# Two attention layers on one core: maxima and scores cut into tiles of 32 rows and 32 columns

## The chip, the cores and the metric

The kernel runs on one core of one Trainium2 chip. The metric is the device time of one execution in microseconds (us). Of the kernel before there are three timed runs: 1005.83, 1009.34 and 1009.84 us, with a median of 1009.34 us.

## The reference

A batch of 32 sequences, `x` of 256 tokens by 320 channels, goes through two cross-attention layers one after the other, each with its own context of 77 tokens by 512 channels and its own weights. Each layer has 20 heads of 16 channels. Cut to what matters:

```
q = heads(x @ Wq); k = heads(ctx @ Wk); v = heads(ctx @ Wv)      # float32
s = einsum('bhqd,bhkd->bhqk', q, k) / sqrt(16)
p = softmax(s, axis=-1)
o = merge(einsum('bhqk,bhkd->bhqd', p, v))
x = o @ Wo + bias + x
```

The reference has further branches for context tokens past the 77th. There are none, so they add nothing. Everything is float32.

## The kernel before, in words

**Units and groups.** Two sequences make a pair; 16 pairs times two layers are 32 units. The 320 channels of the two sequences of a pair are laid out as five groups of 128 rows (`NG = 5`): groups 0 to 3 hold 128 channels of one sequence each, group 4 the last 64 channels of both. A group has 256 query columns and eight heads. Its 128 rows are four quadrants of 32 rows (index `j`), and a quadrant holds two heads (index `e`), 16 rows each. 32 units of five groups make 160 calls each of `maxima`, `scores`, `products` and `divide`.

**The steps of a group.** `queries`/`queries_rest` make q with the group's rows on partitions (through `project`, line 195 with 128 rows and line 184 with 64 rows, and `project_rest`, line 213). `keys`/`keys_rest` (lines 242 and 225) make kT: twice, once for each `e`, with the other head's 16 rows multiplied by zero. Then:

- `maxima` (matmul at line 326) makes, for each quadrant `j` and each half `c` of the queries, a block of 128 queries by 154 columns (two heads by 77 keys) in bank `j` of PSUM. The queries are the stationary operand (a weight load of 32 rows by 128 columns), the keys are streamed. VectorE takes the largest value over the 77 keys (`tensor_reduce`, line 334, one for each bank).
- `turn` (once a unit, after its five maxima) transposes the maxima and writes them by small DMAs into the 16 rows of q that the masked keys leave free; `kM` is kT with -1 in one such row (`tensor_scalar_add` on GpSimd, line 257), so that the next matmul subtracts the maximum.
- `scores` (matmul at line 360) makes 77 keys by 256 queries for each quadrant `j` and head `e`: the keys are the stationary operand (32 rows by 77 columns), the queries are streamed. Quadrant `j` again writes bank `j`, head `e` the half `e` of it. ScalarE takes the exponential of each bank (line 366).
- `products` (matmul at line 380, called by `values`) multiplies by the values: 77 rows by 32 columns of weights, four column tiles beside each other; a column of ones in the values gives the sums. `divide` and `values` turn, divide and turn back (lines 392 to 414).
- `finish`/`finish_rest` (lines 195, 184, 213 again) project the result and `add` (line 421) adds bias and residual.

**Tiles of the array.** A matmul whose operands sit on 32 rows, or whose output has 32 partitions, uses only that part of TensorE's array, and matmuls on different parts can run beside each other. Before the change, `maxima` and `scores` use four row tiles (32 rows, all columns), `products`, `project_rest` and `keys_rest` four column tiles (32 columns, all rows in use), and the other matmuls the whole array, or halves of 64 rows. A float32 matmul of the code appears in the trace as two weight loads and two matmuls, so 160 x 8 calls of line 326 are 2,560 matmuls.

**The order.** The order is written out by hand: each step is put into a numbered slot (`at`), and in a slot the steps run in the order load, maxima, turn, scores, values, rest, full, last. A slot has one group's maxima (for a unit six slots ahead), one group's scores, in every other slot the values of two groups, and projections. Eight PSUM banks are handed out in turn: four to a maxima call, four to a scores call, one to each other step. TensorE takes its instructions in this order; SyncE's queue issues nearly all DMAs.

Of the kernel before, what the change touches and what calls it, by code (L numbers as in the profile page):

```python
# [52 lines left out]
B, S, C, CA, L = 32, 256, 320, 512, 77  # L53
HEADS, HD = 20, 16
P = 128
# [34 lines left out]
def xattn_kernel(ctx: ExitStack, tc: tile.TileContext, xT, cT, cP, weights, outT):  # L90
    nc = tc.nc
# [10 lines left out]
    def bank(name):  # L102
        return psum.tile([P, 512], F32, tag="bank", name=name)
# [45 lines left out]
    for i in range(2):  # L149
        m = const.tile([P, 2 * NG, 32], F32, name=f"max_{i}")  # L150
# [18 lines left out]
    def of_group(x, g):  # L169

        if g < 4:
            return x[:, (g // 2) * NT + (g % 2) * S : (g // 2) * NT + (g % 2 + 1) * S]
        return x[:, 2 * NT : NX]
# [145 lines left out]
    def maxima(u, g):  # L319
        q0, kT, mx = st[u]["q"][0], st[u]["k"], maxes[u % 2]  # L320
        q = of_group(q0, g)
        ps = [bank(f"psm_{u}_{g}_{j}") for j in range(4)]
        for c in range(S // P):
            for j in range(4):
                r = slice(32 * j, 32 * j + 32)
                nc.tensor.matmul(  # L326
                    ps[j][:, c * 2 * L : (c + 1) * 2 * L],
                    q[r, c * P : (c + 1) * P],
                    kT[r, :, g, :],
                    start=True,  # L330
                    stop=True,
                )
        for j in range(4):
            nc.vector.tensor_reduce(  # L334
                mx[:, 2 * g : 2 * g + 2, 2 * j : 2 * j + 2],
                ps[j][:, : 4 * L].rearrange("p (c e k) -> p c e k", e=2, k=L),
                AX.X,
                ALU.max,
            )
# [13 lines left out]
    def scores(u, g):  # L353
        kM = st[u]["km"]
        ps = [bank(f"pss_{u}_{g}_{j}") for j in range(4)]
        for e in range(2):
            q = of_group(st[u]["q"][e], g)
            for j in range(4):
                r = slice(32 * j, 32 * j + 32)
                nc.tensor.matmul(  # L360
                    ps[j][:L, e * S : (e + 1) * S], kM[r, e, g, :], q[r, :],
                    start=True, stop=True,
                )
        st[u]["p", g] = [probs.tile([P, 512], F32, tag="pT", name=f"pT_{u}_{g}_{j}") for j in range(4)]
        for j in range(4):
            nc.scalar.activation(st[u]["p", g][j][:L], ps[j][:L], AF.Exp, scale=SCALE)  # L366
# [84 lines left out]
    for u, (p, layer) in enumerate(units):  # L451
# [22 lines left out]
        for g in range(NG):  # L474
            at(s - 6 + g, "maxima", lambda u=u, g=g: maxima(u, g))
            at(s + g, "scores", lambda u=u, g=g: scores(u, g))
# [120 lines left out]
```

## Time and profile before

| what | value |
|---|---|
| median of three runs | 1009.34 us |
| the profiled execution | 1003.92 us, its span 1002.1 us |
| granted TensorE clock | 1.0 over the whole span |
| TensorE matmuls (PE) | 989.1 us busy, 99% of the span, 12,608 matmuls |
| TensorE weight loads (PEld) | 695.4 us busy, 69%, 12,608 loads |
| VectorE (DVE) | 587.9 us, 59% |
| ScalarE (ACT) | 420.7 us, 42% |
| GpSimd (POOL) | 183.0 us, 18% |
| DMA queue 1 | 23.7% of 16 engines' span |

The profile of one execution names each engine's busy time and groups instructions by line, engine and shapes. "32\*128 32x154" on a matmul means a weight of 32 rows and 128 columns and 154 streamed columns on 32 rows. The busy time of a group is the time in which at least one of its instructions was running; matmuls overlap, so a group's mean duration times its count is far more than its busy time. The chain of waits follows the work back from the last instruction of the program and tells which engine and line held the end.

### The profile page before, as it was taken

How to read it: one execution, taken by the hardware profiler on the slowest of the kernel's cores; microseconds unless marked ns; L12 is line 12 of the kernel's file. 1: busy time of each engine (PE TensorE's matmuls, PEld its weight loads, DVE VectorE, ACT ScalarE, POOL GpSimd, SP SyncE). 2: the span in 40 equal slices, each digit the busy share in tenths (PEclk: the TensorE clock that was granted, in tenths of full speed). 3: DMA queues.
4: the chain of work that ended last, by engine and by line, in shares of the span. 5: the costliest groups of instructions: out<-in, count | busy, mean ns of one | idle time of the engine just before them, and what ended most of it. 6: DMA issues, size and time to landing. Idle time of an engine off the chain costs nothing.

```text
span 1002.1 us, 29771 instructions
## 1 busy us (share of the span) xinstructions
PE 989.1 (99%) x12608; PEld 695.4 (69%) x12608; DVE 587.9 (59%) x1380; ACT 420.7 (42%) x905; POOL 183.0 (18%) x236
## 2 busy tenths in 40 slices
PE   7999999999999999999999999999999999999998
PEld 5666776667776767767677676677666776676755
DVE  2456655566665666555666555665656666566664
ACT  1354434444444434444444444443543444443453
POOL 2111102111120111101111021111201112011111
PEclk9999999999999999999999999999999999999999
DMA  5541222221132311323113132121322212230012
GB/s 207 185 150 40 77 69 95 68 75 66 52 121 68 109 52 42 120 78 118 37 60 101 64 121 69 68 74 58 122 78 72 69 44 94 68 104 30 24 71 80
DMA packets 53894, 82.69 MB, mean 83 GB/s; under 512 B 15556, under 2 KB 35652, under 8 KB 53762
## 3 DMA queue, kind: packets, MB, share of 16 engines
q1 hardware_dynamic: 53330, 78.96, 23.7%
q8 instruction: 99, 1.62, 0.6%
q10 hardware_dynamic: 432, 1.84, 0.5%
q14 instruction: 33, 0.27, 0.1%
HBM read 35.39 MB, written 10.49 MB: 46 GB/s over the span
## 4 chain that ended last, share of the span: by engine, by line
PE 97%; DVE 1%; DMA 1%; SPq 0%; POOL 0%; issue 0%; POOLq 0%
PE po L380 15%; PE pss L360 14%; PE psq L195 12%; PE psy L195 12%; PE psm L326 12%; PE psv L290 9%; PE psk L242 7%; PE psy L213 4%; PE psq L213 4%; PE psy L184 3%; PE psq L184 3%; PE psk L225 2%; DVE max L334 1%; DMA w<-in_w_dram 0%; SPq L347 0%; DVE turned L392 0%
## 5 line engine op out<-in xcount | busy, mean ns | idle before, releaser
L366 ACT ACTIVATE pT<-pss 77x512 f32<-77x512 f32 x640 | 327.1, 592 | 357.8 <-PE pss L360 357.8
L334 DVE TENSOR_REDUCE max<-psm 128x4 f32<-128x308 f32 x640 | 261.4, 471 | 267.6 <-PE psm L326 267.6
L401 POOL TENSOR_TENSOR normal<-turned,inv 128x256 f32<-128x256 f32 x160 | 99.4, 621 | 542.0 <-DVE inv L396 542.0
L360 PE MATMUL pss<-q,kM 32*77 32x256 f32 x2560 | 171.3, 375 | 1.9 <-DMA q<-mT 1.9
L380 PE MATMUL po<-pT,v 77*32 77x256 f32 x2560 | 155.9, 382 | 0.0
L326 PE MATMUL psm<-kT,q 32*128 32x154 f32 x2560 | 130.4, 314 | 1.3 <-DVE max L334 0.8
L326 PEld LDWEIGHTS psm<-kT,q 32*128 32x128 f32 x2560 | 92.9, 183 | 55.8 <-issue 52.6
L257 POOL TENSOR_SCALAR kM<-kT,less 128x385 f32<-128x385 f32 x64 | 80.0, 1263 | 268.9 <-DVE kT L249 268.9
L380 PEld LDWEIGHTS po<-pT,v 77*32 77x32 f32 x2560 | 75.3, 109 | 71.7 <-DVE max L334 28.8
L392 DVE STREAM_TRANSPOSE turned<-po 128x512 f32<-128x512 f32 x160 | 109.5, 684 | 24.3 <-PE po L380 24.3
L195 PE MATMUL psq<-x,w 128*128 128x256 f32 x512 | 123.3, 389 | 0.0
L360 PEld LDWEIGHTS pss<-q,kM 32*77 32x77 f32 x2560 | 109.1, 141 | 15.4 <-issue 3.2
L195 PE MATMUL psy<-oT,w 128*128 128x256 f32 x512 | 119.1, 386 | 0.0
L195 PEld LDWEIGHTS psq<-x,w 128*128 128x128 f32 x512 | 93.3, 190 | 27.1 <-issue 10.8
L195 PEld LDWEIGHTS psy<-oT,w 128*128 128x128 f32 x512 | 94.6, 190 | 22.3 <-issue 10.3
L421 DVE SCALAR_TENSOR_TENSOR x<-psy,w,x 128x256 f32<-128x256 f32 x160 | 72.7, 476 | 43.9 <-PE psy L195 40.7
L290 PE MATMUL psv<-w,cv 128*128 128x320 f32 (+1 forms) x320 | 96.7, 445 | 0.8 <-DVE max L334 0.8
L414 DVE STREAM_TRANSPOSE oT<-normal 128x256 f32<-128x256 f32 x160 | 71.1, 445 | 34.4 <-POOL normal L401 34.4
L290 PEld LDWEIGHTS psv<-w,cv 128*128 128x128 f32 (+1 forms) x320 | 56.2, 185 | 35.9 <-DVE max L334 12.5
L268 ACT COPY q<-psq 128x256 f32<-128x256 f32 x128 | 46.1, 373 | 82.8 <-PE psq L195 70.2
L242 PEld LDWEIGHTS psk<-c,w 128*128 128x128 f32 x512 | 70.2, 193 | 11.6 <-DVE max L334 11.4
L242 PE MATMUL psk<-c,w 128*128 128x154 f32 x512 | 77.6, 305 | 0.0
(28 smaller groups left out, 446.3 us busy)
## 6 DMA issues: line engine op xcount, KB each, us to landing
q<-q SPq DMA_DIRECT2D x32, 640.0 KB
x<-in_xT_dram SPq DMA_DIRECT2D x16, 640.0 KB
c<-in_cP_dram SPq DMA_DIRECT2D x32, 308.0 KB
cv<-in_cT_dram SPq DMA_DIRECT2D x38, 256.0 KB
out_dram<-x SPq DMA_DIRECT2D x15, 640.0 KB
v<-stage SPq DMA_DIRECT2D x26, 192.5 KB
q<-mT SPq DMA_DIRECT2D x256, 5.0 KB
w<-in_w_dram ACTq DMA_DIRECT2D x2, 640.0 KB
```

The source lines that it names most:

```text
L195: nc.tensor.matmul(ps[t][b][:, 0:S], w[:, kc, t * P : (t + 1) * P], x[:, i : i + S], start=(kc == 0 and t < rest), stop=(kc == 1 and t >= ...
L213: nc.tensor.matmul(ps[r, 0:S], lhsT, rhs, start=(kc == 0), stop=(kc == 2))
L242: nc.tensor.matmul(ps[:, 0 : 2 * L], w["k"][:, kc, t * P : (t + 1) * P], c_sb[:, kc, :], start=(kc == 0), stop=(kc == NKA - 1),)
L257: nc.gpsimd.tensor_scalar_add(kM[:, e], kT[:, e], less[:, e : e + 1])
L290: nc.tensor.matmul(ps[:n, :C], c_sb[:, kc, :n], w_sb[layer]["v"][:, kc, :], start=(kc == 0), stop=(kc == NKA - 1),)
L326: nc.tensor.matmul(ps[j][:, c * 2 * L : (c + 1) * 2 * L], q[r, c * P : (c + 1) * P], kT[r, :, g, :], start=True, stop=True,)
L334: nc.vector.tensor_reduce(mx[:, 2 * g : 2 * g + 2, 2 * j : 2 * j + 2], ps[j][:, : 4 * L].rearrange("p (c e k) -> p c e k", e=2, k=L), AX.X ...
L360: nc.tensor.matmul(ps[j][:L, e * S : (e + 1) * S], kM[r, e, g, :], q[r, :], start=True, stop=True,)
L366: nc.scalar.activation(st[u]["p", g][j][:L], ps[j][:L], AF.Exp, scale=SCALE)
L380: nc.tensor.matmul(po[32 * j : 32 * j + 32, e * S : (e + 1) * S], vpad[:L, b, pair, e].rearrange("p a d -> p (a d)"), pT[j][:L, e * S : (e ...
L392: nc.vector.transpose(turned[:, 0 : 2 * S], po)
L401: nc.gpsimd.tensor_tensor(normal.rearrange("p q e d -> p e q d"), outs, inv.unsqueeze(3).broadcast_to([P, 2, S // 32, HD]), ALU.mult,)
```

## The change

Two steps issue their matmuls in another cut; nothing else is touched. `maxima` cuts the 128 stationary queries of each block into four pieces of 32 (index `m`), each of which writes 32 partitions of the same bank. `scores` cuts the 77 stationary keys into 32, 32 and 13. The streamed columns of each matmul, 154 and 256, stay as they were. A maxima call issues 32 matmuls of the code instead of 8, a scores call 24 instead of 8. The piece `m` is the outer loop and the quadrant `j` the inner one.

```diff
         for c in range(S // P):
-            for j in range(4):
-                r = slice(32 * j, 32 * j + 32)
-                nc.tensor.matmul(
-                    ps[j][:, c * 2 * L : (c + 1) * 2 * L],
-                    q[r, c * P : (c + 1) * P],
-                    kT[r, :, g, :],
-                    start=True,
-                    stop=True,
-                )
+            for m in range(4):
+                for j in range(4):
+                    r = slice(32 * j, 32 * j + 32)
+                    n = c * P + 32 * m
+                    nc.tensor.matmul(
+                        ps[j][32 * m : 32 * m + 32, c * 2 * L : (c + 1) * 2 * L],
+                        q[r, n : n + 32],
+                        kT[r, :, g, :],
+                        start=True,
+                        stop=True,
+                    )
...
         for e in range(2):
             q = of_group(st[u]["q"][e], g)
-            for j in range(4):
-                r = slice(32 * j, 32 * j + 32)
-                nc.tensor.matmul(
-                    ps[j][:L, e * S : (e + 1) * S], kM[r, e, g, :], q[r, :],
-                    start=True, stop=True,
-                )
+            for m in range(0, L, 32):
+                n = min(m + 32, L)
+                for j in range(4):
+                    r = slice(32 * j, 32 * j + 32)
+                    nc.tensor.matmul(
+                        ps[j][m:n, e * S : (e + 1) * S], kM[r, e, g, m:n], q[r, :],
+                        start=True, stop=True,
+                    )
```

## The prediction

> **What bounds the kernel now.** I read the page's busy times first, then the chain of waits, then the groups of the two changed lines, then the timeline of one slot, and last the table of busy times by stretch, which I use as a counter.
>
> ```profile
> PE 989.1 (99%) x12608; PEld 695.4 (69%) x12608; DVE 587.9 (59%) x1380; ACT 420.7 (42%) x905; POOL 183.0 (18%) x236
> ...
> q8 instruction: 99, 1.62, 0.6%
> ...
> PE 97%; DVE 1%; DMA 1%; SPq 0%; POOL 0%; issue 0%; POOLq 0%
> ...
> L360 PE MATMUL pss<-q,kM 32*77 32x256 f32 x2560 | 171.3, 375 | 1.9 <-DMA q<-mT 1.9
> L326 PE MATMUL psm<-kT,q 32*128 32x154 f32 x2560 | 130.4, 314 | 1.3 <-DVE max L334 0.8
> L326 PEld LDWEIGHTS psm<-kT,q 32*128 32x128 f32 x2560 | 92.9, 183 | 55.8 <-issue 52.6
> ```
>
> TensorE is the chain (97%), and its matmuls wait for almost nothing (1.9 and 1.3 us in 160 calls each). So the change is worth what it does to TensorE's own pace. The same place in a slot, by the timeline of TensorE's matmuls:
>
> ```profile
> 504.64 0.38 PE L195 MATMUL psq<-x,w 128*128 128x256 f32 x1
> 504.95 0.81 PE L326 MATMUL psm<-kT,q 32*128 32x154 f32 x16
> 505.58 1.04 PE L360 MATMUL pss<-q,kM 32*77 32x256 f32 x16
> 506.55 0.42 PE L380 MATMUL po<-pT,v 77*32 77x256 f32 x4
> ```
>
> A maxima call takes 0.63 us to the first scores, a scores call 0.97 us to the next line. To see what is in that, I count the matmuls of line 326 that have started by a given time (the number after x):
>
> ```profile
> 504.94:504.95 0.01, 0.00 (x1) 1.00 0.00 0
> ...
> 504.94:504.97 0.03, 0.02 (x4) 1.00 0.00 0
> 504.94:505.18 0.24, 0.23 (x4) 1.00 0.00 0
> ...
> 504.94:505.21 0.27, 0.26 (x8) 1.00 0.00 0
> 504.94:505.31 0.37, 0.36 (x8) 1.00 0.00 0
> 504.94:505.35 0.41, 0.40 (x12) 1.00 0.00 0
> 504.94:505.44 0.51, 0.49 (x12) 1.00 0.00 0
> 504.94:505.48 0.54, 0.53 (x16) 1.00 0.00 0
> ```
>
> The sixteen start in fours, one of each row tile, at 504.95, 505.185, 505.32 and 505.45: 0.235 us after the first four, then 0.133 us each. Inside a four the starts lie about 7 ns apart (four in about 20 ns). So the four tiles do run beside each other, a four costs 0.133 us of streaming 154 columns, and only the first one costs 0.10 us more. The same counting gives the scores' fours 0.215 us apart from the first, and the values' (32-column weights) 0.240 and then 0.215.
>
> **The change, part by part.** *Streaming.* Each new tile streams as many columns as the old one. If all sixteen run together, the call is still 2 halves x 2 passes = four rounds of 0.133 us, and scores still four rounds of 0.215 us: nothing gained or lost. More tiles only divide the stationary side, which was not what took the time.
>
> *The first weight load, removed in part.* Before a maxima call the array changes its tiling (whole array to row tiles) and stands empty, so the first load is bare: 0.235 - 0.133 = 0.10 us for 128 columns. For 32 columns the values' row gives 0.240 - 0.215 = 0.025 us. I take that: 0.077 us x 160 = 12.3 us less. Bounds: nothing, if sixteen loads in a row cost as much as four wide ones, to 16 us, if it goes altogether. Between maxima and scores there is no bare load now (0.133 us from the last four to the scores) and none after.
>
> *The staggered end, added.* A tile's two loads and two matmuls are fed before the next tile's, and the next tile starts 7 ns later. In scores the last of twelve tiles then runs 11 x 6.7 = 73 ns behind the first, instead of 3 x 6.7 = 20 ns. The next line has another tiling and waits for the array to empty (the scores' last four starts at 506.23 us and streams to 506.45, the values' first load comes at 506.55), so it starts behind the last tile: 0.053 us x 160 = 8.5 us more. Bounds: 0 to 16 us (double). Between maxima and scores the stagger costs nothing, since each tile goes straight on.
>
> *Feeding.* Maxima and scores together now hold 224 instructions (128 + 96, loads and matmuls) in place of 64, in about 1.42 us: 6.3 ns each. Shown by the trace: after a wait with nothing queued, at 39.52 us, the first weight loads of the next scores come like this (count of loads of line 360; the stretches end at 39.530, 39.562, 39.569 and 39.575):
>
> ```profile
> 39.50:39.53 0.03, 0.01 (x1) 1.00 0.00 0
> 39.50:39.56 0.06, 0.04 (x2) 1.00 0.00 0
> 39.50:39.57 0.07, 0.04 (x3) 1.00 0.00 0
> 39.50:39.58 0.07, 0.05 (x4) 1.00 0.00 0
> ```
>
> Four instructions in 6.7 ns is 1.7 ns each, over one tile after another. Over a longer run the densest stretch is the chain's
>
> ```profile
> 508.49 0.54 PE psk L225 x32
> ```
>
> which is 64 instructions in 0.54 us, 8.4 ns each, and there streaming sets the pace (77 columns, eight fours). So the price lies between 0 and (8.4 - 6.3) x 224 = 0.47 us a group, 75 us in all. I take 0, since 1.7 ns is the only row that is not itself held by streaming. The code grows from 1.62 MB by about as much again; the instruction queue goes from 0.6% to about 1.2% of the DMA time, which nothing waits for.
>
> *Semaphores.* Line 360 also has 160 semaphore instructions of 51 ns on TensorE's queue, five a unit, hidden behind maxima's 0.63 us now. With more instructions queued in the same time they come later; 0 to 5 x 0.051 x 32 = 8 us, I take 1 us.
>
> *Off the path.* Bank `j` is complete when its last piece is: 0.025 + 4 x 0.133 + 12 x 0.0067 = 0.64 us, as now (0.10 + 0.53). VectorE's reduction (261 us) and ScalarE's exponential (327 us) keep their times, and both engines are under 60% busy. No DMA, wait or buffer is moved.
>
> *Sum.* -12.3 + 8.5 + 0 + 1 = -2.8 us on the profiled execution: 1003.9 to 1001.1 us. The median of the runs shown is 5.4 us above that execution, so 1009.3 - 2.8 = **1006.5 us**.
>
> A rule against this change: the Trainium skill, "TensorE: Matmul & The Clock Gate", section "Wait — 56ns, not 53.3ns?", says that matmuls never start closer than about 25 ns. By it, as an estimate, 64 starts make 1.6 us for maxima and 48 make 1.2 us for scores, +1.2 us a group and some +190 us. The starts 7 ns apart above speak against it for matmuls on different tiles; no row shows sixteen. Another rule points the other way: in the same page, "Measured speedup vs the span model" gives 10.6 times for sixteen tiles and 4 ns from tile to tile; by it the stagger would cost 5.1 us and the sum be about -6 us. No row here shows that either.
>
> **The rivals.** *Feeding is the new bound* (slower). The mechanism is in the line of instructions ahead of TensorE in maxima and scores; it decides once an instruction takes more than 6.3 ns over 224. For it: no row shows 64 instructions in less than 0.54 us. Against: the 1.7 ns above, with an empty queue. At the 8.4 ns of the densest row it costs 0.47 us a group, 75 us: 1085 us; with part of it queued ahead, 1030 to 1085.
>
> *Sixteen do not run together* (the change does not do what it says). If the four pieces of one row quadrant share one line of work, a piece can start only when the one ahead of it is in its second pass. Maxima then takes 8 x (0.133 + 0.025) + 0.133 = 1.40 us instead of 0.63, scores 6 x (0.215 + 0.025) + 0.215 = 1.66 instead of 0.97 us: +1.46 us a group, 234 us, 1243 us. For it: rows show four row tiles or four column tiles, never both at once. Against: both kinds keep four separate lines, and the values' four column tiles stream from the same rows at the full 0.215 us, so neither reading nor loading the same rows is in the way.
>
> *The stagger is free* (faster). If the next tiling waits for less than the last tile, or the tiles close up, the 8.5 us fall away: 1003.9 - 11.3, on the runs 998 us.
>
> **How the numbers follow.** Sixteen together with the sum above, -5 to +5 us: 0.42. The stagger free or the load gain larger, more than 5 us faster: 0.18. Feeding or semaphores, 5 to 85 us slower: 0.23. Not together, around 1243 us: 0.17. A measurement of this kernel tells about 0.5% (5 us) from no change, so faster 0.18, same 0.42, slower 0.40. The range 996 to 1085 us leaves out the last case alone; the likeliest case by itself is 1002 to 1012 us.
>
> **What would show it.** 10,240 matmuls of line 326 with weights of 32 columns, 7,680 of line 360. Right: sixteen starts within about 0.11 us, 0.56 us from the first maxima matmul to the first scores, about 1.03 us from there to the next line, both lines together 3 us less in the chain. Feeding: starts in a round further apart than 8 ns, rounds of maxima longer than 0.133 us. Not together: starts in fours that are 0.13 us or more apart. The prediction is wrong if the rounds themselves become longer, or if VectorE's reductions come up in the chain.

## The result and the profile after

The changed kernel takes 1100.7 us (median; 1100.24 to 1102.94). The ratio to the kernel before is 1.0947, with a 95% interval from 1.0915 to 1.0979: **9.5% slower**, 93 us (with a fourth run, the median of the kernel before is 1007.6 us). The forecast was 1006.5 us, the range ended at 1085 us. The profiled execution has a span of 1099.1 us against 1002.1, 97 us more, and the granted clock is 1.0 throughout, as before. Later runs of the kernel before took 1003.3 to 1004.4 us where the granted clock was 1.0 and 1005.9 to 1010.0 us where it was 0.993 to 0.998, so differences of a few us are read below from the spans of the profiled executions, all at 1.0.

The page of the changed kernel, the lines that answer to those of before (maxima is now line 328, scores line 364):

```profile
PE 1085.9 (99%) x25408; PEld 759.1 (69%) x25408; DVE 589.2 (54%) x1380; ACT 420.0 (38%) x905; POOL 182.7 (17%) x236
...
q8 instruction: 199, 3.26, 1.2%
...
PE 98%; DVE 1%; DMA 1%; SPq 0%; issue 0%; POOL 0%; POOLq 0%
...
L364 PE MATMUL pss<-q,kM 32*32 32x256 f32 (+1 forms) x7680 | 239.2, 379 | 1.5 <-DMA q<-mT 1.5
...
L328 PE MATMUL psm<-kT,q 32*32 32x154 f32 x10240 | 187.9, 300 | 2.0 <-issue 1.3
L328 PEld LDWEIGHTS psm<-kT,q 32*32 32x32 f32 x10240 | 118.3, 103 | 75.8 <-issue 53.9
```

The added time lies in the two changed lines and nowhere else: busy time of the maxima matmuls 130.4 to 187.9 us, of scores 171.3 to 239.2 us, 125 us together with their overlaps counted twice, while the other matmul lines (products 155.9 and 155.7 us, the q projections of line 195 123.3 both times), VectorE, ScalarE and GpSimd keep their busy times and the matmuls still wait for almost no other engine. One slot on TensorE, in the timeline:

```profile
563.83 1.03 PE L328 MATMUL psm<-kT,q 32*32 32x154 f32 x55
564.56 0.40 PE L364 MATMUL pss<-q,kM 32*32 32x256 f32 x1
564.56 0.37 PE L328 MATMUL psm<-kT,q 32*32 32x154 f32 x6
564.65 0.37 PE L364 MATMUL pss<-q,kM 32*32 32x256 f32 x1
564.66 0.32 PE L328 MATMUL psm<-kT,q 32*32 32x154 f32 x3
564.79 1.34 PE L364 MATMUL pss<-q,kM 32*32 32x256 f32 x46
566.06 0.40 PE L242 MATMUL psk<-c,w 128*128 128x154 f32 x1
```

From the first maxima matmul to the first of scores it is 0.73 us (0.63 before; 0.56 forecast), from there to the next line 1.50 us (0.97 before; about 1.03 forecast). Over all calls of the two traces the medians are 0.73 and 1.47 us, against 0.63 and 0.97 before: 0.60 us a group, 96 us in 160 groups, nearly all of the 97. The last maxima even start after the first scores. The counter shows where it stops, first for the matmuls of line 328 from the call's start at 563.827:

```profile
563.82:563.93 0.12, 0.11 (x16) 1.00 0.00 0
563.82:563.98 0.16, 0.15 (x16) 1.00 0.00 0
563.82:564.09 0.27, 0.26 (x32) 1.00 0.00 0
563.82:564.16 0.34, 0.34 (x32) 1.00 0.00 0
563.82:564.17 0.35, 0.35 (x33) 1.00 0.00 0
563.82:564.29 0.47, 0.47 (x33) 1.00 0.00 0
563.82:564.30 0.48, 0.47 (x34) 1.00 0.00 0
563.82:564.33 0.51, 0.50 (x36) 1.00 0.00 0
563.82:564.40 0.58, 0.57 (x40) 1.00 0.00 0
```

then for its weight loads:

```profile
563.82:563.99 0.17, 0.16 (x33) 1.00 0.00 0
563.82:564.17 0.35, 0.26 (x33) 1.00 0.00 0
563.82:564.18 0.36, 0.27 (x34) 1.00 0.00 0
563.82:564.30 0.48, 0.36 (x34) 1.00 0.00 0
563.82:564.31 0.49, 0.37 (x35) 1.00 0.00 0
563.82:564.33 0.51, 0.38 (x36) 1.00 0.00 0
563.82:564.34 0.52, 0.40 (x38) 1.00 0.00 0
563.82:564.36 0.54, 0.42 (x40) 1.00 0.00 0
```

Here too, a number after x counts what has started. The first half of the call goes just as forecast: sixteen tiles start within 0.11 us, and their second passes start from 0.16 us on, 32 matmuls and 32 loads by 0.27 us. Sixteen tiles do run together. Then there is a hole. One load more (the 33rd) goes at once; the 33rd matmul, tile 0's first of the second half, could start when its tile is free at 0.16 + 0.133 = 0.29 us and starts at 0.345. The 34th follows only at 0.475, and the next tile's load behind it. From there on the tiles come 17 ns apart (loads 36 to 40, two to a tile, in 0.035 us), not 7 ns. This is no single case: over the 160 calls of the trace the 33rd matmul comes 0.341 us and the 34th 0.474 us after the first (medians).

**The queue theory.** 32 loads and 32 matmuls are 64 instructions. If TensorE holds 64 instructions in program order, and a place comes free only when the instruction 64 places earlier has finished, the hole follows. The first matmul of tile 0 ends its streaming at 0.16 us, and its place is taken at 0.345, 0.18 us later; the second ends at 0.29, and its place is taken at 0.475, again 0.18 later. (The 34th alone would prove little, since the 33rd streams on the same tile until about 0.475. But the 35th load, for the next tile, whose matmuls had streamed by 0.30 us, is held until then too.) With new places filled at 17 ns for four instructions (4.2 ns each), scores then start 60 instructions after that, at 0.475 + 0.25 = 0.73 us, which is what the timeline shows. By this theory sixteen tiles with four instructions each use up all 64 places, so no tile has its next job waiting; before the change, maxima and scores together were 64 instructions, and every tile's next job was in the queue. The Trainium skill, "TensorE: Matmul & The Clock Gate", gives an "Engine queue depth" of 64 in its first table; the hole behind the 64th instruction agrees with it. I had not weighed it in the prediction.

**Rivals.** The price theory: each instruction has a price (93 us over the 25,600 added ones, 3.6 ns), wherever it stands. The sharing theory: tiles that share rows or columns of the array disturb one another.

### The profile page after: what moved, and what is told of

It is laid out like the page before. It is cut to its first block, busy times and chain, and to the rows that moved or that the text cites. A ratio compares the mean times of both kernels' runs of the same rounds, so it can differ in the third digit from the quotient of the medians.

```text
span 1099.1 us, 55457 instructions
## 1 busy us (share of the span) xinstructions
PE 1085.9 (99%) x25408; PEld 759.1 (69%) x25408; DVE 589.2 (54%) x1380; ACT 420.0 (38%) x905; POOL 182.7 (17%) x236
## 4 chain that ended last, share of the span: by engine, by line
PE 98%; DVE 1%; DMA 1%; SPq 0%; issue 0%; POOL 0%; POOLq 0%
PE pss L364 17%; PE psm L328 15%; PE po L384 13%; PE psq L195 11%; PE psy L195 11%; PE psv L290 9%; PE psk L242 7%; PE psy L213 4%; PE psq L213 4%; PE psq L184 3%; PE psy L184 3%; PE psk L225 2%; DMA w<-in_w_dram 0%; DVE turned L396 0%; SPq L349 0%
## 5 line engine op out<-in xcount | busy, mean ns | idle before, releaser
L364 PE MATMUL pss<-q,kM 32*32 32x256 f32 (+1 forms) x7680 | 239.2, 379 | 1.5 <-DMA q<-mT 1.5
L328 PE MATMUL psm<-kT,q 32*32 32x154 f32 x10240 | 187.9, 300 | 2.0 <-issue 1.3
L328 PEld LDWEIGHTS psm<-kT,q 32*32 32x32 f32 x10240 | 118.3, 103 | 75.8 <-issue 53.9
L364 PEld LDWEIGHTS pss<-q,kM 32*32 32x32 f32 (+1 forms) x7680 | 148.6, 97 | 21.8 <-issue 10.9
L384 PE MATMUL po<-pT,v 77*32 77x256 f32 x2560 | 155.7, 382 | 0.0
L195 PE MATMUL psq<-x,w 128*128 128x256 f32 x512 | 123.3, 389 | 0.0
```

What stands on the lines that cost most here:

```text
L195: nc.tensor.matmul(ps[t][b][:, 0:S], w[:, kc, t * P : (t + 1) * P], x[:, i : i + S], start=(kc == 0 and t < rest), stop=(kc == 1 and t >= ...
L328: nc.tensor.matmul(ps[j][32 * m : 32 * m + 32, c * 2 * L : (c + 1) * 2 * L], q[r, n : n + 32], kT[r, :, g, :], start=True, stop=True,)
L364: nc.tensor.matmul(ps[j][m:n, e * S : (e + 1) * S], kM[r, e, g, m:n], q[r, :], start=True, stop=True,)
L384: nc.tensor.matmul(po[32 * j : 32 * j + 32, e * S : (e + 1) * S], vpad[:L, b, pair, e].rearrange("p a d -> p (a d)"), pT[j][:L, e * S : (e ...
```

## The experiments

The two parts alone, first. **Only maxima** in 32 x 32; the diff is that of scores against the changed kernel:

```diff
-            for m in range(0, L, 32):
-                n = min(m + 32, L)
-                for j in range(4):
+            for j in range(4):
...
-                        ps[j][m:n, e * S : (e + 1) * S], kM[r, e, g, m:n], q[r, :],
+                    ps[j][:L, e * S : (e + 1) * S], kM[r, e, g, :], q[r, :],
```

> Only maxima in tiles of 32 rows and 32 columns; scores as before. Queue theory: TensorE holds 64 instructions in program order and a place comes free only when the instruction 64 places earlier has finished, so a tile's next job (128 instructions a call) starts late; maxima alone costs about 0.37 us a group, and the change of tiling between maxima and scores (0.09 us empty plus 0.06 us bare load) is part of it: 1007 + 85 = about 1090 us. Instruction-price theory (93 us spread over 25,600 added instructions, 3.6 ns each): 15,360 are added, 56 us, plus 25 us for the change of tiling: about 1088 us. Sharing theory (sixteen tiles disturb each other): rounds of maxima longer than 0.133 us while sixteen run.

Measured: 1083.85 us, ratio 1.0780 (1.0742 to 1.0818). Its slot:

```profile
546.66 1.16 PE L328 MATMUL psm<-kT,q 32*32 32x154 f32 x64
547.74 1.10 PE L362 MATMUL pss<-q,kM 32*77 32x256 f32 x16
548.78 0.64 PE L382 MATMUL po<-pT,v 77*32 77x256 f32 x8
```

Maxima to scores 1.08 us instead of 0.63, of which 0.09 is the array running empty for the new tiling; scores 1.04 instead of 0.97 (the bare load of 77 columns that was hidden before). The queue theory and the price theory both give this time within 7 us, so the run does not tell them apart. **Only scores**, the diff that of maxima against the changed kernel:

```diff
-            for m in range(4):
-                for j in range(4):
+            for j in range(4):
...
-                        ps[j][32 * m : 32 * m + 32, c * 2 * L : (c + 1) * 2 * L],
-                        q[r, n : n + 32],
+                    ps[j][:, c * 2 * L : (c + 1) * 2 * L],
+                    q[r, c * P : (c + 1) * P],
```

> Only scores in tiles of 32 rows and 32 columns; maxima as before. Queue theory: twelve tiles of four instructions fill 48 of 64 places, so the loss is smaller than in maxima, and a change of tiling (0.09 us empty, 0.025 us bare load) comes in between: 1007 + 68 = about 1075 us. Instruction-price theory: 10,240 added, 37 us, plus 18 us for the tiling: about 1062 us. Sharing theory: scores' rounds longer than 0.215 us for each tile.

Measured: 1063.54 us, ratio 1.0575 (1.0543 to 1.0607). That is nearer to the price theory (1062) than to the queue theory (1075). Its slot:

```profile
520.18 0.81 PE L326 MATMUL psm<-kT,q 32*128 32x154 f32 x16
520.91 1.34 PE L362 MATMUL pss<-q,kM 32*32 32x256 f32 x48
522.19 1.93 PE L382 MATMUL po<-pT,v 77*32 77x256 f32 x32
```

Maxima to scores 0.73 us (0.63 before), scores 1.28 us (0.97 before). What the two runs do show together: 78.0 + 57.7 = 136 us of loss for the parts, 93 for the whole. The difference, 43 us, fits the tiling that now changes between maxima and scores in both: (0.09 + 0.06) + (0.09 + 0.025) us, times 160, is 42 us.

**Eight tiles of 64 columns** keeps the idea and halves the tiles. Scores' second piece is made 33 columns wide, so that both pieces are of one tiling (no run has a piece of 13 columns beside one of 64, so whether this was needed is not shown); the last 20 of them lie over the next keys (kM becomes one row of 770 columns and 20 more) and their results are not read. Maxima first, then scores:

```diff
-            for m in range(4):
+            for m in range(2):
...
-                        ps[j][32 * m : 32 * m + 32, c * 2 * L : (c + 1) * 2 * L],
-                        q[r, n : n + 32],
+                        ps[j][64 * m : 64 * m + 64, c * 2 * L : (c + 1) * 2 * L],
+                        q[r, n : n + 64],
...
-            for m in range(0, L, 32):
-                n = min(m + 32, L)
+            for m, n in ((0, 64), (64, 97)):
...
+                    at_k = (e * NG + g) * L
...
-                        ps[j][m:n, e * S : (e + 1) * S], kM[r, e, g, m:n], q[r, :],
+                        ps[j][m:n, e * S : (e + 1) * S], kM[r, at_k + m : at_k + n], q[r, :],
```

> Both in tiles of 32 rows and 64 columns, eight at a time: maxima in two pieces of 64 queries, scores in keys 0 to 63 and a piece of 33 columns (the 13 left and 20 that are not read). Queue theory: eight tiles of four instructions take 32 of 64 places, so every tile's next job is in the queue in time and nothing is lost; the bare load falls from 0.10 to 0.053 us (-8 us) and the staggered end grows by 4 x 6.7 ns (+4 us): about 1003 us, 4 us faster than before. Instruction-price theory: 10,240 added instructions at 3.6 ns, 37 us: about 1040 us. Sharing theory: eight tiles, two on the same rows, somewhere between: 1020 to 1060 us.

Measured: 1002.55 us, ratio 0.9965 (0.9948 to 0.9982): the queue theory's number, far from the 1040 us of the price theory and the 1020 to 1060 us of the sharing theory. That the number is met so closely is in part luck: at the same clock the spans are 1000.9 us and 1002.1 before, so the gain is 1.2 us and not the 4 that were expected. The version has 17,728 matmuls and as many loads, exactly as many as the run with scores alone, and is 61 us faster; the tiling change explains 18 of that. A price for each instruction cannot give this. The slot:

```profile
504.58 0.78 PE L331 MATMUL psm<-kT,q 32*64 32x154 f32 x32
505.16 1.07 PE L367 MATMUL pss<-q,kM 32*64 32x256 f32 x32
506.16 1.93 PE L387 MATMUL po<-pT,v 77*32 77x256 f32 x32
```

Maxima 0.58 us (0.63 before): the bare load is 0.05 us shorter. Scores 1.00 us (0.97 before): the last tile is some 0.03 us further behind. Over all calls the medians are 0.577 and 1.016 us against 0.630 and 0.970, so the two nearly cancel.

**The same instructions in another order.** The halves `c` become the innermost loop of maxima, so that the two jobs of a tile stand side by side.

```diff
-        for c in range(S // P):
-            for m in range(4):
-                for j in range(4):
+        for m in range(4):
+            for j in range(4):
+                for c in range(S // P):
```

> The changed kernel with the loop over the two halves of the queries innermost in maxima: the same matmuls on the same tiles, the same number of instructions, only the two jobs of a tile stand next to each other. Queue theory: a tile now has eight instructions in a row, so 64 places hold eight tiles and not sixteen; maxima and scores together lose another 0.5 us a group: about 1180 us. Instruction-price theory: no difference, 1101 us. Sharing theory: fewer tiles at once, so rather faster than 1101 us.

Measured: 1171.21 us, ratio 1.1645 (1.161 to 1.168). Number, shapes and tiles of the matmuls are those of the changed kernel; only their order differs, and it costs 70 us more. The price theory had no difference, the sharing theory rather a gain. The counter for line 328, from a call's start at 560.765:

```profile
560.76:560.87 0.11, 0.10 (x8) 1.00 0.00 0
560.76:560.92 0.16, 0.15 (x8) 1.00 0.00 0
560.76:561.02 0.27, 0.26 (x16) 1.00 0.00 0
560.76:561.05 0.29, 0.28 (x16) 1.00 0.00 0
560.76:561.10 0.34, 0.34 (x20) 1.00 0.00 0
```

Where sixteen tiles had started by 0.11 us, eight have, and no ninth up to 0.29 us: eight tiles of eight instructions are 64. This is the clearest evidence that the places are counted in program order, whatever the tiles are doing. The trace shows the wait itself: the 17th to 20th matmul come 13 ns apart, as second jobs of the first four tiles would, and the 21st breaks this step and comes 0.340 us after the first (median), as late as the 33rd of the changed kernel (0.341). Taken as the ninth tile's first, it is again the 66th instruction. In both runs it starts 27 to 28 ns after the recorded end of the 2nd instruction, in 159 of 160 calls.

**Tiles of 32 by 32, but eight at a time**, to part the width of a tile from the number of tiles; the loops of maxima and of scores:

```diff
-            for m in range(4):
+            for m in range(2):
...
-            for m in range(0, L, 32):
-                n = min(m + 32, L)
+            for m in range(0, 64, 32):
+                n = m + 32
```

> The changed kernel's tiles of 32 by 32, but only eight of them at a time: maxima of the first two pieces only (half of the queries have no maximum) and scores of 64 of the 77 keys; reductions, exponentials and products follow on 64 partitions. It leaves that work out, and no streamed column is saved for it, since all tiles of a row quadrant run beside each other. Queue theory: eight tiles of four instructions fit twice into 64 places, nothing is lost: 7 us less than before from the shorter bare load, and some 7 us more because products on 64 rows is now another tiling than the steps after it: about 1006 us. Instruction-price theory: 10,240 instructions more than before, 37 us: about 1043 us. A theory that tiles of 32 columns are slow in themselves: near 1100 us.

Measured: 1009.18 us, ratio 1.0022 (1.0004 to 1.0041), 3 us above the queue theory and 34 below the price theory. At the same clock the spans are 1007.3 us and 1002.1 before: 5 us longer, where the queue theory's sum has no change. In the counter, the rounds of eight come without a hole:

```profile
507.51:507.59 0.07, 0.07 (x8) 1.00 0.00 0
507.51:507.67 0.15, 0.15 (x8) 1.00 0.00 0
507.51:507.74 0.23, 0.22 (x16) 1.00 0.00 0
507.51:507.80 0.28, 0.28 (x16) 1.00 0.00 0
507.51:507.87 0.35, 0.35 (x24) 1.00 0.00 0
507.51:507.94 0.42, 0.42 (x24) 1.00 0.00 0
507.51:508.00 0.48, 0.48 (x32) 1.00 0.00 0
```

So the 32-column tile is not slow in itself.

**Where narrow tiles do pay.** The 64-column version showed one gain: a narrower weight makes the bare load after a change of tiling shorter, which there the later end of scores all but took back. The last run adds that to the 64-column version for the whole-array matmuls, with few enough tiles for the queue. The diff shows `project`; `keys` and `vals` are cut in the same way.

```diff
-                    nc.tensor.matmul(
-                        ps[t][b][:, 0:S], w[:, kc, t * P : (t + 1) * P], x[:, i : i + S],
...
+                    for m in range(0, P, 32):
+                        nc.tensor.matmul(
+                            ps[t][b][m : m + 32, 0:S], w[:, kc, t * P + m : t * P + m + 32], x[:, i : i + S],
```

> The version with tiles of 64 columns in maxima and scores, and also the whole-array matmuls of the projections, keys and values cut into four column tiles of 32 (the 64-row ones stay). Queue theory: four tiles of four instructions are 16 of 64 places, nothing is lost there; about 150 bare loads a run become 0.025 instead of 0.10 us (-12 us), and the ends stagger by 0.02 us (+3 us): about 993 us, 1.2% faster than before. Instruction-price theory: some 11,000 instructions more than the 64-column version: about 1040 us.

Measured: 995.12 us, ratio 0.9881 (0.9853 to 0.9909), the fastest of all versions, with 23,248 matmuls instead of the 12,608 of before. At the same clock the spans are 993.0 us, 1000.9 in the 64-column version and 1002.1 before: 9 us or 0.9% less than before, 8 of them from this step (9 were expected). The counter for the projection after a change of tiling, in the 64-column version (one whole-array matmul at a time, from 509.62):

```profile
509.61:509.93 0.32, 0.30 (x1) 1.00 0.00 0
509.61:509.95 0.34, 0.33 (x2) 1.00 0.00 0
```

and here (fours, from 505.19):

```profile
505.19:505.42 0.23, 0.23 (x4) 1.00 0.00 0
505.19:505.45 0.27, 0.26 (x8) 1.00 0.00 0
```

The second round comes 0.32 us after the first with 128-column weights and about 0.24 us with four loads of 32 columns, against 0.215 us of streaming: 0.105 us bare there, 0.025 here.

## Why the prediction was wrong, point by point

- **Streaming, right for the first two rounds only.** "If all sixteen run together, the call is still four rounds": they do run together, and the first two rounds start at 0 and 0.16 us as worked out. The step was carried on to the later rounds without asking whether their instructions would be there.
- **Feeding, the step that failed.** I put it at 0 "since 1.7 ns is the only row that is not itself held by streaming". That row counted four loads, some 13 instructions, too few to fill 64 places, and TensorE stood there waiting for a DMA (1.60 us in the trace), so the queue need not have been empty, as the prediction takes it to be. The row shows how fast instructions leave the queue, not how fast places in it come free. Free places are refilled at 4.2 ns an instruction in the changed kernel. Even that is below the 6.3 ns that the price bound asked for; what costs is that they come free 64 instructions later and only 0.18 us after a matmul has streamed. Where the prediction has 0, the traces show a loss of 0.60 us a group, 96 us in all, with the small gains and losses of the other terms in it. The feeding rival had the right place and a wrong price (75 us, from 8.4 ns an instruction), so the range fell 16 us short.
- **"The stagger costs nothing between maxima and scores"** held only in the first half; from the 65th instruction on, tiles follow 17 ns apart instead of 7.
- **The first weight load** was sized rightly: with eight tiles of 32 columns, maxima to scores is 0.080 us shorter than before (medians of 0.550 and 0.630 us; 0.077 was forecast), with 64 columns 0.053 us.
- **The staggered end** was put too low: at 6.7 ns for a tile, the four more tiles of the 64-column version should cost scores 0.027 us, and they cost 0.046. Load and end together leave that version 1.2 us faster. In the changed kernel the hole hides what they are worth.
- **"Sixteen do not run together"** was wrong (1243 us), and so was the stagger coming free. The semaphores' 1 us cannot be told apart in these runs.
- **Off the path** held: TensorE is 98% of the chain (97% before), VectorE 1% both times.
- **The 25 ns rule** that the prediction takes from the skill's page, and that would have given about 1200 us, is not what happens on separate tiles: sixteen starts within 0.11 us are 7 ns apart. They are not the 4 ns apart of its other rule either.

The number 64 can be read off the trace of the changed kernel, if each tile's instructions are taken in the order load, matmul, load, matmul. The 33rd load, the 65th instruction, starts 0.159 us after the first matmul (median), while the 2nd instruction is still running; the 33rd matmul, the 66th, is held until 27 to 28 ns after the 2nd has ended. With 63 places the 65th would have been held by the 2nd, and with 65 the 66th would have been held only by the 1st, a load that had ended by 0.11 us, and could have started when its tile was free, at 0.29 us.

What stays open: no run changed the number of places itself; the recorded ends of matmuls are modelled, so what exactly frees a place is not shown; and why new places fill at 4.2 ns an instruction is not shown either. The queue theory's numbers fit the six runs within 12 us; those for the two parts alone and for the other order were 6 to 12 us too high.

## What to carry to other kernels

Before a step is cut into more tiles, count its instructions between two jobs of the same tile: here a float32 matmul is four, and with 64 of them in between no tile has its next job waiting. Half as many tiles cost nothing. Tiles on the same streamed data save no streaming; what they save is the bare weight load after a change of tiling (0.10 us at 128 columns, 0.025 at 32), and they put off the end of the step (0.046 us for four more tiles in scores). So cut narrowly where a tiling begins, into few tiles, and keep neighbouring steps in one tiling (0.09 us and a bare load for each change).

## What the runs showed of the hardware

The order of issue matters for matmuls on separate tiles, even with nothing to wait for: the same matmuls, re-ordered, took 70 us more. All sixteen 32 by 32 tiles do stream float32 side by side at the full pace, while the queue holds their instructions: their second passes begin 0.157 us after the first ones, 0.133 us for 154 columns and 0.025 us for the bare load. And nearly twice as many matmuls and loads (23,248 of each against 12,608) can run faster: a span of 993.0 against 1002.1 us.
